# First h transposed ahead of the last score weights, x of pair 1 loaded by SyncE with its norm made beside the score matrix, column sums in a tile of their own

## The chip, the cores and the metric

The kernel runs on one core of one Trainium2 chip. The metric is the device time of one execution in microseconds (us), as the median of several runs. A profile is taken of one further execution; all moments given below are counted from the start of that execution's span.

## The reference

There are B = 128 graphs with N = 128 nodes and D = 512 features, all in float32. Two layers follow each other, each added to its input:

```
h = relu(layernorm(x))                                   # layer 0
Xw = h @ Wv + bv
e  = leaky_relu(Xw@aw[:d] over columns + Xw@aw[d:] over rows + ab, 0.2)
T  = adj * exp(e), each row divided by its sum
H  = h @ Wk[0] + bk[0] + (T h) @ Wk[1] + bk[1] + (T T h) @ Wk[2] + bk[2]
x  = x + relu(H)

h = relu(layernorm(x))                                   # layer 1
q, k = split(h @ Wqk);  v = h @ Wv1
w = mask/sqrt(512) * sum_d(q * (adj @ (k * mask)))
x = x + softmax_over_nodes(w) * v
```

Layer 1 needs q and k only in the product q·(adj k), so the kernel makes one 512 x 512 matrix Wq Wk^T ahead of everything else (the "score matrix") and uses it in place of the two.

## The kernel before, in words

Graphs are handled in 64 pairs (`G = 2`). For each pair p, layer 0 runs two block products after Strassen's scheme, seven products in place of eight (`strassen`, L371): `y2(p)` with the right side `r2` (Wk[2], with one column of attention weights on either side, 514 columns in all) and `y10(p)` with the right side `r10` (Wk[1] and Wk[0]). Their left side is h of the pair, transposed, and four sums of its blocks (`left_sums`). Their right side needs four differences of weight blocks each (`combine`, L191). Then come the two multiplications by the transition matrix (`inner`, `outer`), the layer norm of layer 1 (`norm2`) and the stores to DRAM that the second stage reads back. The second stage (from the closing of the first stage's buffers at L840) runs over quads of pairs and takes the last three eighths of the time.

The change touches the start, before the loop over pairs, and one choice in the loop.

**Loads.** SyncE (SP) issues x of pair 0, the four row chunks of Wqk (tile `tl`, 512 KB each), and the first two of four row blocks of Wv, Wk[2], Wk[1] and Wk[0] (`rows`, L166; tiles named `t`, `w`, `r` in the profile, 256 KB each, each filling 32 partitions). GpSimd (POOL) waits for chunk 1 of Wqk by means of a small copy, `gate` (L174), and then issues x of pair 1 and the other two row blocks of each matrix. Each queue also waits, before each issue, until an earlier transfer that used the same semaphore has landed. adj of pairs 0 and 1 comes last on both.

**TensorE (PE) up to the loop.** Two short warm-up groups; `weights_transposed` (L261), which transposes the four chunks of Wqk through six PSUM banks, each chunk into two banks of four transposes, copied out as `wqt` and `wkt`; `transposed_by_pe` (L351) for h of pair 0, through banks a2 and e2, which the chunks use as well; a transpose of the mask (`masks`), a small sum (`attention_constant`), the bias row spread over partitions (`bias`, bank c1); `score_matrix` (L276), 32 matmuls; `y2(0)`; two spreads of a column (L186); then `y10(0)` and the loop.

**VectorE (DVE) and ScalarE (ACT).** DVE makes the attention columns (`attention_columns`, L230), eight multiply-and-sum instructions over Wv, whose sums go straight into the two outer columns of `r2`, the tile that the loads of Wk[2] also fill. It then makes the differences for `r2`, the statistics of x of pair 1, and the differences for `r10`. ACT normalizes pair 1 (`norm0(1)`, L403, in two instructions at L316) as a step inside `y2(0)`, after its product 6. SP then stores h of pair 1 and reads it back in blocks.

**The order.** The program is written against a planner (Tile) that puts the instructions of each engine in an order of its own, from estimated times; the program pins it by hand where it wants: `tc.issue_after(done[...])`, `behind(...)` and `ordered(...)` (which chains PE instructions through `done["mm"]`) put an instruction behind a named earlier one of the same engine.

**One choice in the loop.** In `strassen` (L388) ACT copies bank a to bank b after the first product; the third product, on bank b, adds to that copy. The argument `second` names an instruction that this copy is put behind. In `y10(p)` (L600) it is `h2`, the last normalizing instruction of layer 1's norm of the pair before, for all p but the first and the last.

## Time and profile before

| what | us |
|---|---|
| runs of the kernel | 2225.20, 2225.92, 2229.39 (median 2225.92) |
| the profiled execution, its own time | 2229.96 |
| its span, first to last instruction | 2228.2 |
| PE busy in the span | 2205.7 (99%) |
| DVE, ACT, POOL busy | 1672.1, 1235.8, 698.6 |
| Wqk chunk 3 reaches PE | 13.35 |
| first score-matrix matmul | 16.78 |
| first matmul of y2(0) | 30.62 |
| first matmul of y10(0) | 38.52 |

The profile lists, for each instruction or run of like instructions, the start in us, the duration in us (of the whole run, where several are merged), the engine, the source line, the operation and its tiles as out<-in, the number of instructions, and in brackets how long the engine had been idle and what ended that. PE and PEld are matmuls and weight loads of TensorE; a matmul in float32 is listed as two. L91 and L86 are lines inside the helpers `ordered` and `behind`, so that many instructions stand under them. The words DMA, SPq and POOLq stand for transfers and for their issue.

### The profile page before, as it was taken

To read this page: it belongs to the slowest core of one execution; us is meant where nothing else is said; L and a number is where in the kernel's file an instruction comes from. 1 tells how busy PE (TensorE), PEld (TensorE's weight loads), DVE (VectorE), ACT (ScalarE), POOL (GpSimd) and SP (SyncE) were. 2 spreads that over 40 slices of the span, in tenths; PEclk is the share of its full clock that TensorE was granted. 3 is DMA by queue.
4 is the path that set the end of the run, shared out by engine and by line. 5 is a ranking of instruction groups with operands and counts; after the bars stand their busy time and mean duration, and the time that the engine had idled before them with its cause. 6 is when DMAs were issued, how large, how long until landed. Compare 5 with 4: busy or idle time off the path is not lost.

```text
span 2228.2 us, 29421 instructions
## 1 busy us (share of the span) xinstructions
PE 2205.7 (99%) x8113; PEld 1535.0 (69%) x8113; DVE 1672.1 (75%) x4529; ACT 1235.8 (55%) x2858; POOL 698.6 (31%) x822
## 2 busy tenths in 40 slices
PE   9999999999999999999999999999999999999998
PEld 5666665656666665666666666688888878887886
DVE  5778777778787777877778787587777767777777
ACT  4555554455554555545555554456666666666664
POOL 3111111111121211212112121245555555555454
PEclk9999999999999999999999999999999999999999
DMA  7688788888787887878778786668888888888876
GB/s 208 181 243 244 230 266 248 266 271 246 225 239 222 238 238 220 244 227 232 234 227 241 218 245 211 250 205 239 223 262 226 237 223 256 235 227 242 239 219 179
DMA packets 425615, 519.35 MB, mean 233 GB/s; under 512 B 100310, under 2 KB 281174, under 8 KB 409578
## 3 DMA queue, kind: packets, MB, share of 16 engines
q1 hardware_dynamic: 383880, 391.84, 58.1%
q0 software_dynamic: 41280, 125.09, 21.6%
q8 instruction: 65, 1.06, 0.2%
q14 instruction: 100, 0.82, 0.1%
q10 hardware_dynamic: 290, 0.53, 0.1%
HBM read 295.26 MB, written 222.07 MB: 232 GB/s over the span
## 4 chain that ended last, share of the span: by engine, by line
PE 90%; DVE 4%; DMA 3%; SPq 1%; ACT 1%; issue 1%; DVEq 0%
PE a L91 26%; PE c L91 24%; PE b L91 24%; PE e L91 15%; DMA td<-t 2%; DMA hv<-h2d 1%; SPq L534 1%; DVE st L290 0%; DMA tl<-in_L_gnn_Wqk_dram 0%; DVE fw L427 0%; DVE z L86 0%; SPq L342 0%; DVE x L621 0%; DMA xg<-in_x_dram 0%; SPq L86 0%
## 5 line engine op out<-in xcount | busy, mean ns | idle before, releaser
L669 POOL TENSOR_TENSOR c<-s,c 128x512 f32<-128x512 f32 (+1 forms) x186 | 201.0, 1094 | 250.2 <-DVE s L669 244.9
L111 POOL DMA_DIRECT2D agb<-in_adj_dram x256 | 149.7, 591 | 338.8 <-DVE aT L86 251.8
L91 PE MATMUL a<-r,x 128*128 128x512 f32 x512 | 242.4, 596 | 0.1
L91 PE MATMUL b<-rw,in 128*128 128x256 f32 x884 | 212.0, 379 | 0.0
L91 PEld LDWEIGHTS b<-rw,in 128*128 128x128 f32 x884 | 168.0, 190 | 23.3 <-issue 0.5
L435 POOL DMA_DIRECT2D fd<-fw x62 | 34.7, 559 | 464.3 <-DVE fw L443 278.0
L91 PEld LDWEIGHTS a<-r,x 128*128 128x128 f32 x512 | 97.6, 191 | 96.8 <-issue 93.4
L86 ACT COPY s<-c 128x257 f32<-128x257 f32 (+1 forms) x128 | 61.5, 481 | 173.4 <-PE c L91 173.2
L86 ACT COPY b<-a 128x257 f32<-128x257 f32 (+1 forms) x128 | 59.3, 464 | 171.6 <-PE a L91 171.6
L86 DVE TENSOR_TENSOR e<-e,s 128x512 f32<-128x512 f32 x64 | 44.7, 699 | 143.5 <-ACT s L86 143.5
L669 POOL TENSOR_TENSOR c<-c 128x1024 f32<-128x1024 f32 x61 | 144.1, 2362 | 11.2 <-DVE c L669 10.9
L91 PE MATMUL a<-w,x 128*128 128x257 f32 x512 | 131.9, 380 | 0.1
L91 PE MATMUL b<-w,sx 128*128 128x257 f32 x512 | 132.0, 380 | 0.0
L91 PE MATMUL b<-t,sx 128*128 128x512 f32 x256 | 120.4, 592 | 1.2 <-ACT b L86 1.2
L91 PE MATMUL c<-t,sx 128*128 128x512 f32 x256 | 120.5, 593 | 0.2
L91 PE MATMUL b<-r,sx 128*128 128x512 f32 x256 | 120.3, 592 | 0.0
L91 PE MATMUL e<-t,sx 128*128 128x512 f32 x256 | 120.3, 592 | 0.0
L91 PE MATMUL c<-t,x 128*128 128x512 f32 x256 | 120.3, 592 | 0.0
L669 DVE SCALAR_TENSOR_TENSOR junk<-agg,wscale,c 128x512 f32<-128x512 f32 x126 | 97.1, 770 | 29.9 <-POOL c L669 24.6
L669 ACT ACTIVATE c<-c,wcol 128x512 f32<-128x512 f32 x124 | 86.3, 720 | 56.7 <-DVE wcol L669 56.7
L427 DVE STREAM_TRANSPOSE fw<-hv 128x256 f32<-128x256 f32 x248 | 88.1, 413 | 30.1 <-DMA hv<-h2d 29.7
L91 PE MATMUL a<-rw,f 128*128 128x256 f32 x448 | 108.1, 379 | 0.0
(265 smaller groups left out, 5258.1 us busy)
## 6 DMA issues: line engine op xcount, KB each, us to landing
fd<-fw POOLq DMA_DIRECT2D x62, 1024.0 KB, 5.1
x1d<-x SPq DMA_DIRECT2D x64, 512.0 KB, 4.2
h2d<-h SPq DMA_DIRECT2D x64, 512.0 KB, 3.7
xg<-in_x_dram SPq DMA_DIRECT2D x63, 512.0 KB, 7.1
hd<-h SPq DMA_DIRECT2D x63, 512.0 KB, 3.6
hv<-hd SPq DMA_DIRECT2D x252, 128.0 KB, 4.2
hv<-h2d SPq DMA_DIRECT2D x248, 128.0 KB, 4.1
h<-h2d SPq DMA_DIRECT2D x62, 512.0 KB, 8.4
```

The source lines that it names most:

```text
L86: return op(*args, **how)
L91: done["mm"] = op(*args, **how).ins
L111: nc.gpsimd.dma_start(agb[p][c * S32:(c + 1) * S32].rearrange("p g q i -> p (g q) i"), v[c])
L427: done["c12"] = nc.vector.transpose(blocks[:, k, j].rearrange("p f (n b) -> p f n b", n=Q), hv[:, j].rearrange("p n (k f a) -> p k f n a", ...
L435: nc.gpsimd.dma_start(fd[:, half].rearrange("p o n -> p (o n)"), fv[:, half].rearrange("p o n -> p (o n)"))
L534: done["tv"] = nc.sync.dma_start(tv[c * S32:(c + 1) * S32].rearrange("p g q i -> p (g q) i"), v[c]).ins
L669: done[engine] = op(*args, **how).ins
```

## The change

- In the loads: SP issues x of pair 1 itself, right after the four chunks of Wqk and ahead of its weight rows; POOL no longer loads it, and its gate now waits for chunk 2 of Wqk.
- On PE: chunks 0 to 2 of Wqk are transposed first, then h of pair 0 (now in banks a1 and b1), the mask and the bias (now in bank b2), and only then chunk 3. All of these are now chained with `ordered`. Of the copies out of PSUM for `wkt`, ACT now does chunk 2 alone and DVE does chunks 0, 1 and 3.
- The statistics of x of pair 1 come on DVE behind the copies of the weights, and the norm (`norm0(1)`) behind the last copy of `wqt` on ACT, beside the score matrix; it is no longer a step of `y2(0)`. The differences for `r10` are put behind those for `r2`.
- The attention columns are put behind the left sums, their sums go to a new tile `ucol` (128 x 2 x 4), and two small copies, which are new, bring them into `r2`.
- In the loop, the copy in `y10(1)` is no longer put behind `h2`; for pair 2 and later it still is.

```diff
     for c in range(DC):
         nc.sync.dma_start(wqk_sb[:, c], wqk[c * P:(c + 1) * P])
+    load_x(1)
...
-    done["gate"] = nc.gpsimd.tensor_copy(gate, wqk_sb[:, 1, :1]).ins
+    done["gate"] = nc.gpsimd.tensor_copy(gate, wqk_sb[:, 2, :1]).ins
...
     with tc.issue_after(done["gate"]):
-        load_x(1, nc.gpsimd)
...
+        ucol = setup.tile([P, 2, DC], FP, name="ucol")
...
-                    junk, wv0_sb[:, f], 1.0, aw_bc[:, a, :], op0=OP.mult, op1=OP.mult, accum_out=r2[:, f, a * (W2 + HD):a * (W2 + HD) + 1]).ins
+                    junk, wv0_sb[:, f], 1.0, aw_bc[:, a, :], op0=OP.mult, op1=OP.mult, accum_out=ucol[:, a, f:f + 1]).ins
+        for a in range(2):
+            at = a * (W2 + HD)
+            done["u"] = behind("u", nc.vector.tensor_copy, r2[:, :, at:at + 1], ucol[:, a, :, None]).ins
...
-        nc.tensor.transpose(c1[:, :B], nm, ident[:B, :B])
+        ordered(nc.tensor.transpose, c1[:, :B], nm, ident[:B, :B])
...
-        nc.tensor.matmul(c1, ones[:K, :], bkr, start=True, stop=True)
-        nc.scalar.copy(bias_a[:, 1], c1[:, :HD])
-        nc.vector.tensor_sub(bias_e[:, 1], c1[:, HD:], bias_a[:, 1])
-
-    def weights_transposed():
+        ordered(nc.tensor.matmul, b2, ones[:K, :], bkr, start=True, stop=True)
+        nc.scalar.copy(bias_a[:, 1], b2[:, :HD])
+        nc.vector.tensor_sub(bias_e[:, 1], b2[:, HD:], bias_a[:, 1])
+
+    def weights_transposed(chunks):
...
-                    (nc.vector.tensor_copy if c < HC else nc.scalar.copy)(wkt[:, :, c * P:(c + 1) * P], pt)
+                    done["wk"] = (nc.scalar.copy if c == HC else nc.vector.tensor_copy)(wkt[:, :, c * P:(c + 1) * P], pt).ins
...
-            second="h2" if 0 < p < NP - 1 else "warm")
+            second="h2" if 1 < p < NP - 1 else "warm")
...
-    with tc.issue_after(done["vector"]):
-        weights_transposed()
+    done["mm"] = done["vector"]
+    weights_transposed(range(HC + 1))
     hT0 = lefts.tile([P, G, DC, N], FP, name="x")
-    transposed_by_pe(h0, hT0, (a2, e2))
+    transposed_by_pe(h0, hT0, (a1, b1))
     masks()
     behind("rs", attention_constant)
     bias()
-    attention_columns()
+    weights_transposed(range(HC + 1, DC))
+    rs1 = behind("wk", statistics, xg[1], "wq")
     LEFT[0] = left_sums(hT0)
-    with tc.issue_after(done["u"]):
-        right2 = combine(halves(r2, W2), [t2[:, i] for i in range(4)])
+    behind("left", attention_columns)
     for p in range(2):
         load_adj(p)
     for f in range(Q):
         score_matrix(f)
-    rs1 = behind("right", statistics, xg[1])
-    with tc.issue_after(done["rs"]):
+    behind("wq", norm0, 1, rs1)
+    with tc.issue_after(done["u"]):
+        right2 = combine(halves(r2, W2), [t2[:, i] for i in range(4)])
+    with tc.issue_after(done["right"]):
         right10 = combine(halves(r10, HD), pairs(t10))
     with tc.issue_after(done["right"]), tc.issue_after(done["m"]):
-        y2(0, {6: lambda: behind("s", norm0, 1, rs1)})
+        y2(0)
```

More of the change, by code (lines that the diff above doesn't have):

```diff
@@ L254, in bias @@
     def bias():
-        nc.tensor.matmul(c1, ones[:K, :], bkr, start=True, stop=True)
-        nc.scalar.copy(bias_a[:, 1], c1[:, :HD])
-        nc.vector.tensor_sub(bias_e[:, 1], c1[:, HD:], bias_a[:, 1])
-    def weights_transposed():
+        ordered(nc.tensor.matmul, b2, ones[:K, :], bkr, start=True, stop=True)
+        nc.scalar.copy(bias_a[:, 1], b2[:, :HD])
+        nc.vector.tensor_sub(bias_e[:, 1], b2[:, HD:], bias_a[:, 1])
+    def weights_transposed(chunks):
         banks = [a2, e2, a1, b1, c1, e1]
-        for c in range(DC):
+        for c in chunks:
             for a in range(2):
@@ L269, in weights_transposed @@
                     at = a * D + o * P
-                    nc.tensor.transpose(pt[:, o, :], wqk_sb[:, c, at:at + P], ident)
+                    ordered(nc.tensor.transpose, pt[:, o, :], wqk_sb[:, c, at:at + P], ident)
                 if a:
-                    (nc.vector.tensor_copy if c < HC else nc.scalar.copy)(wkt[:, :, c * P:(c + 1) * P], pt)
+                    done["wk"] = (nc.scalar.copy if c == HC else nc.vector.tensor_copy)(wkt[:, :, c * P:(c + 1) * P], pt).ins
                 else:
-                    nc.scalar.copy(wqt[:, :, :, c, :], pt.rearrange("p o (f a) -> p o f a", f=Q))
+                    done["wq"] = nc.scalar.copy(wqt[:, :, :, c, :], pt.rearrange("p o (f a) -> p o f a", f=Q)).ins
     def score_matrix(f):
@@ L355, in transposed_by_pe @@
             for f in range(Q):
-                nc.tensor.transpose(pt[:, f, :], h[:, j, f * P:(f + 1) * P], ident)
+                ordered(nc.tensor.transpose, pt[:, f, :], h[:, j, f * P:(f + 1) * P], ident)
             (nc.vector.tensor_copy if j else nc.scalar.copy)(dst[:, j], pt)
```

## The prediction

> **What bounds the kernel now.** I read the page first, then PE's waits, then the timeline around each wait that the diff touches.

> ```profile
> span 2228.2 us, 29421 instructions
> PE 2205.7 (99%) x8113; PEld 1535.0 (69%) x8113; DVE 1672.1 (75%) x4529; ACT 1235.8 (55%) x2858; POOL 698.6 (31%) x822
> ```

> PE is busy for all but 22.5 us. No edit takes work off PE, so the change can win only what it closes of those 22.5 us, and whatever is closed at the start moves all the rest forward. PE's waits, of the first 100 us and then of 250 to 450 us (total, times, longest, in us):

> ```profile
> PE a L270 <- DMA tl<-in_L_gnn_Wqk_dram: 1.4, 1, 1.4
> PE b L91 <- ACT b L86: 1.2, 1, 1.2
> ...
> PE a L186 <- ACT y L458: 1.0, 1, 1.0
> ```

> ```profile
> PE c L91 <- ACT s L86: 5.4, 4, 2.0
> PE a L91 <- DVE tt L86: 1.8, 2, 1.2
> ```

> The first three are the places that the diff touches, 3.6 us in all; the second fence is not touched. The first wait, in PE's timeline:

> ```profile
> 11.12 0.78 PE L270 MATMUL e<-ident,tl 128*128 128x128 f32 x4
> 13.35 0.63 PE L270 MATMUL a<-ident,tl 128*128 128x128 f32 x4 [1.44 <-DMA tl<-in_L_gnn_Wqk_dram]
> ...
> 14.25 0.27 PE L250 MATMUL c<-ident,nm 128*128 128x128 f32 x1
> 14.36 0.50 PE L245 MATMUL e<-ccol,ones 128*128 128x1 f32 x4
> 14.73 0.64 PE L356 MATMUL a<-ident,h 128*128 128x128 f32 x4
> 15.20 0.60 PE L356 MATMUL e<-ident,h 128*128 128x128 f32 x4
> 15.73 1.12 PE L257 MATMUL c<-bkr,ones 3*128 3x512 f32 x2
> 16.78 0.70 PE L280 MATMUL a<-wkt,wqt 128*128 128x512 f32 x1
> ```

> PE has nothing from 11.9 to 13.35, since chunk 3 of Wqk is late, and then does work that was ready long before (ACT finished h of pair 0 at 10.47). The other two waits, in ACT's part of the timeline:

> ```profile
> 36.27 1.52 ACT L316 ACTIVATE h<-xg,rs 128x512 f32<-128x512 f32 x2 [0.58 <-DVE rs L304]
> ...
> 37.69 0.35 ACT L458 COPY y<-c 128x257 f32<-128x257 f32 x1
> ...
> 38.10 0.32 PE L186 MATMUL a<-ident,y 128*128 128x128 f32 x1 [0.98 <-ACT y L458]
> ```

> ```profile
> 69.49 0.20 ACT L296 ACTIVATE r<-r 128x2 f32<-128x2 f32 x1
> 70.72 1.52 ACT L316 ACTIVATE h<-x,rs 128x512 f32<-128x512 f32 x2 [1.02 <-DVE rs L304]
> 72.14 0.58 ACT L86 COPY b<-a 128x512 f32<-128x512 f32 x1
> ```

> In both, ACT normalizes a pair for 1.52 us while PE waits for a copy queued behind it. The column sums on DVE:

> ```profile
> 21.51 0.69 DVE L235 SCALAR_TENSOR_TENSOR junk<-t,aw_bc 128x512 f32<-128x512 f32 x1 [2.99 <-DMA t<-in_L_gnn_Wv_dram]
> ...
> 24.50 0.69 DVE L235 SCALAR_TENSOR_TENSOR junk<-t,aw_bc 128x512 f32<-128x512 f32 x1 [2.29 <-issue]
> ```

> Wv is complete at 21.4; the second sum waits until the last row block of Wk[2] has landed (24.32), because it writes into the tile being loaded.

> [...] SP's transfers land in order of issue. [...] The row blocks fill 32 partitions each; [...] 206 GB/s from 10 to 14 us, when the rows run mostly from one queue, 276 GB/s from 14 to 30 us with two. [...] PE starts at half rate[...]. The trace shows it in durations: one group of four transposes starts every 0.86 us up to 11 us, and 0.46 us apart from 13.35; the idle 1.44 us did not slow it again.

> **The change part by part.**

> 1. *h, mask and bias ahead of chunk 3.* Before, from PE's restart to the score matrix: chunk 3 0.90 (13.35 to 14.25), mask 0.11, constant 0.37, h 1.00, bias 1.05, in all 3.43 us, to 16.78. After, PE goes on at about 11.9 (chunks 0 to 2 set this: they run at the cold rate without a gap), with banks a1 and b1 copied out by 11.42 and 11.2. Mask, h and bias take 2.16: 14.1. By then chunk 3 is there (13.35 before; nothing is put ahead of it). It takes 0.90: 15.0. But now its copies stand between it and the score matrix: the wkt copy on DVE takes 0.69 and some 0.2 to 0.3 for the two hand-overs (before, from the end of the last transpose's issue to the ACT copy 0.25): 15.95. Before, that copy hid behind h and bias. If the constant, 0.37, falls ahead of chunk 3 it is 16.3; in PE's new bubble of 0.95 it is free. Gain 16.78 - 15.95 = 0.85, ends 0.3 (a left sum of 0.42 runs on DVE when the copy is due, and the constant is ahead) and 1.3 (chunk 3 earlier, warm rate sooner). Taken: 0.9.
> 2. *Norm of pair 1 beside the score matrix.* ACT is idle from 17.3 to 20.5, beside the score matrix, so 1.52 + 0.50 for the logarithm and exponential fit there. In y2(0) the copy y<-c (0.35) then starts 0.2 after its product (36.83), at 37.03 in place of 37.69: gain 0.66 of the 0.98. The store and the four read-backs of h (0.37 + 1.80 us of issue on SP) come earlier; they wait behind SP's rows and adj in the ring and are needed only at 48.5, so they cost nothing; with that cover gone each us would be one us.
> 3. *Copy in y10(1) free of h2.* Product a ends at 69.74 by issue, the copy could start at 70.0 and ACT is idle from 69.69 to 70.72: a copy of 0.58 fits exactly. Gain 1.16; the norm behind it loses nothing. With the norm first after all, the 1.16 stays.
> 4. *x of pair 1 to SP, gate on chunk 2, ucol.* 512 KB move from POOL's ring to SP's, 2 us go by until POOL's gate opens (8.10 to about 10.2). POOL's first bytes came 5.8 us after its issue, and its ring then moved some 190 KB per us: Wv's 512 KB there by 19 at the latest, from 21.4. SP's half of Wv comes behind x of pair 1, at some 100 to 200 KB per us, by 18. Then DVE: eight sums of 0.73 = 5.9, two copies of 0.16 (nearest row: 128 x 4 at 0.16), four differences 2.63: done by 28 in place of 32.1. PE reaches y2(0) at about 29.7 (15.9 + 13.84), so none of it is on the path; the point at which it would be is Wv at 23.2. r10 landed last at 30.2; it is needed at 35.8, so POOL's two microseconds are covered by more than 5. Cost 0, ends -0.2 (a hand-over of DVE at 52.0 that PE just waits for goes away, since the r10 differences no longer run from 36.86 to 41.6) and +1.
> 5. *Rest.* `ordered`, the bank of the bias and the ucol tile add no instruction to PE. 0.2 gained for the hand-over at 52.0.

> Sum: 0.9 + 0.66 + 1.16 + 0.2 = 2.9 us. The profiled execution goes from 2229.96 (span 2228.2) to about 2227 (2225.3). That execution was 4.0 above the median of 2225.92; the saving is taken from the median: 2223.0, ratio 0.9987. Three runs spread over 4.2 us, and 0.2% (4.45 us) is about what a measurement of this kernel can tell from no change.

> **The rivals.** *B, one of the gains does not come.* The planner may still put the norm ahead of the copy in y10(1), since it stands ahead in the program and only the gap of 1.02 us makes room; or the constant and a left sum delay the score matrix. For it: nothing now pins that order. Against it: the copy was ready 0.7 us before the norm in the trace. Saving 1.2 to 2: about 2224.3. *C, more than the sum.* The waits at 250 to 450 us come from a round trip of the transition blocks through DRAM; they add to 7.2 us, and a moved start could shift them against the transfers. With two or three gone, 2219.5. Against it: they recur inside one pair's work, which the start doesn't change. *D, slower.* The same round trip, the other way: the planner orders the loop anew from its shifted start, and the wait of 1.2 us appears in more pairs. It decides from (2.9 + 4.45) / 1.2 = 6 to 7 further pairs; at ten it is 2225.9 - 2.9 + 12 = 2235. For it: six such waits exist already. Against it: the loop's order is pinned by hand, and between 80 and 260 us PE hardly waits.

> **How the numbers follow.** The sum as forecast 0.62, of which 0.15 falls beyond the bound by run spread and the upper ends of items 1 to 4; B 0.19; C 0.12; D 0.07. So faster by over 0.2% 0.27 (0.15 + 0.12), within 0.2% 0.66 (0.47 + 0.19), slower 0.07. The likeliest case has 2220.5 to 2225.5 for itself; with B and most of C the range is 2218.5 to 2227.

> **What would show it.** Right: no wait of `PE a L270` on tl; h's transposes (L356) before 13.5; the score matrix near 15.9 and y2(0) near 29.7; no wait of the spread above 0.4; no wait of `PE b L91` near 70; y10(1) some 1.7 us earlier, pair 2 some 2.9. Wrong: the score matrix at 16.3 or later, the norm still ahead of the copy, the last r2 difference after 30, or more waits on `ACT s` and `DVE tt` than six in the loop.

## The result, and the profile after

The changed kernel takes 2224.75 us at the median (14 runs, 2222.47 to 2227.22), the kernel before 2227.30 in the runs beside it (2225.20 to 2235.40). The ratio is put at 0.9984, 95% interval 0.9977 to 0.9992: 1.8 to 5.1 us less, in the middle 3.6, clear of no change. (The two medians lie 2.6 us apart, which is inside that interval.) Forecast were 0.9987 and 2223.0 us.

The page of the changed kernel, its first lines; PE is again busy all but 20 us:

```profile
span 2223.8 us, 29417 instructions
PE 2204.0 (99%) x8113; PEld 1535.0 (69%) x8113; DVE 1668.8 (75%) x4532; ACT 1236.0 (56%) x2857; POOL 697.9 (31%) x821
```

PE's waits in the first 100 us (total, times, longest, in us). The three that the prediction named are gone. The first line below stood there before too; the second is new:

```profile
PE e L221 <- DVE ones L158: 1.1, 1, 1.1
PE a L284 <- DVE wkt L276: 0.9, 1, 0.9
```

Between 250 and 450 us, which no edit touches, it waits as long as before (7.4 us, before 7.2), in more and shorter pieces:

```profile
PE c L91 <- ACT s L86: 7.1, 7, 1.5
PE a L91 <- DVE tt L86: 0.3, 1, 0.3
```

PE's timeline at the start, with the new order: h at 11.98, then mask, constant, bias, and chunk 3 at 14.47:

```profile
11.98 0.62 PE L91 MATMUL a<-ident,h 128*128 128x128 f32 x4
...
13.42 1.12 PE L91 MATMUL b<-bkr,ones 3*128 3x512 f32 x2
14.47 0.66 PE L91 MATMUL a<-ident,tl 128*128 128x128 f32 x4
14.96 0.60 PE L91 MATMUL e<-ident,tl 128*128 128x128 f32 x4
16.48 3.67 PE L284 MATMUL a<-wkt,wqt 128*128 128x512 f32 x8 [0.92 <-DVE wkt L276]
...
36.52 0.27 PE L186 MATMUL a<-ident,y 128*128 128x128 f32 x1
36.63 1.02 PE L91 MATMUL a<-r,x 128*128 128x512 f32 x2
37.49 0.27 PE L186 MATMUL a<-ident,y 128*128 128x128 f32 x1
37.60 1.02 PE L91 MATMUL a<-r,x 128*128 128x512 f32 x2
38.46 1.88 PE L91 MATMUL e<-t,sx 128*128 128x512 f32 x4
```

ACT's timeline beside the score matrix and at the end of y2(0): the norm of pair 1 is done long before the copy y<-c, which now starts 0.20 us after the first spread:

```profile
24.99 1.52 ACT L320 ACTIVATE h<-xg,rs 128x512 f32<-128x512 f32 x2 [3.54 <-DVE rs L308]
...
36.72 0.38 ACT L462 COPY y<-c 128x257 f32<-128x257 f32 x1 [1.36 <-PE c L91]
```

And at y10(1); the copy b<-a now goes ahead of the norm, into the gap that it had:

```profile
67.22 0.20 ACT L300 ACTIVATE r<-r 128x2 f32<-128x2 f32 x1
67.66 0.57 ACT L86 COPY b<-a 128x512 f32<-128x512 f32 x1 [0.24 <-PE a L91]
68.44 1.52 ACT L320 ACTIVATE h<-x,rs 128x512 f32<-128x512 f32 x2 [0.21 <-DVE rs L308]
```

Where the time came from, read as starts of the same PE instruction in the two profiles:

| PE instruction | before | after | gained so far | gained in this stretch |
|---|---|---|---|---|
| first of the score matrix | 16.78 | 16.48 | 0.30 | 0.30 |
| first of y2(0) | 30.62 | 30.29 | 0.33 | 0.03 |
| second product of y10(0) | 40.31 | 38.46 | 1.85 | 1.52 |
| first of y2(1) | 52.99 | 50.71 | 2.28 | 0.43 |
| first of y10(1) | 68.02 | 65.75 | 2.27 | -0.01 |
| third product of y10(1) | 72.77 | 69.18 | 3.59 | 1.32 |

So 3.6 us are gained by 73 us in these two profiles, in the middle of the measured interval. The spans differ by 4.4; the rest came and went in the loop and is treated in the last section. The first row is the least sure: the start up to the score matrix is the same in a second profile of the changed kernel and in four of the runs below, and in these six the score matrix begins between 16.05 and 16.81. The second profile of the changed kernel has 16.81 there, and its third product of y10(1) starts at 69.51, so that 3.3 us are gained by then. Of the kernel before there is one profile.

### The profile page after: what moved, and what is told of

Its sections match the earlier page's. It is cut to its first block, busy times and chain, and to the rows that moved or that the text cites. A ratio compares the mean times of both kernels' runs of the same rounds, so it can differ in the third digit from the quotient of the medians.

```text
span 2223.8 us, 29417 instructions
## 1 busy us (share of the span) xinstructions
PE 2204.0 (99%) x8113; PEld 1535.0 (69%) x8113; DVE 1668.8 (75%) x4532; ACT 1236.0 (56%) x2857; POOL 697.9 (31%) x821
## 4 chain that ended last, share of the span: by engine, by line
PE 90%; DMA 4%; DVE 4%; SPq 1%; issue 1%; ACT 1%; DVEq 0%; ACTq 0%
PE a L91 26%; PE c L91 24%; PE b L91 24%; PE e L91 15%; DMA td<-t 2%; DMA hv<-h2d 2%; SPq L538 1%; DVE st L294 1%; DVE fw L431 1%; SPq L346 0%; DVE x L625 0%; DVE z L86 0%; DMA h2d<-h 0%; DMA xg<-in_x_dram 0%; PE a L284 0%
## 5 line engine op out<-in xcount | busy, mean ns | idle before, releaser
L91 PE MATMUL a<-r,x 128*128 128x512 f32 x512 | 240.8, 592 | 0.0
L91 PE MATMUL b<-rw,in 128*128 128x256 f32 x884 | 212.0, 379 | 0.0
L91 PEld LDWEIGHTS b<-rw,in 128*128 128x128 f32 x884 | 168.0, 190 | 23.3 <-issue 0.5
L91 PEld LDWEIGHTS a<-r,x 128*128 128x128 f32 x512 | 97.0, 190 | 95.7 <-issue 92.3
L86 ACT COPY s<-c 128x257 f32<-128x257 f32 (+1 forms) x128 | 61.5, 481 | 173.3 <-PE c L91 173.2
L86 ACT COPY b<-a 128x257 f32<-128x257 f32 (+1 forms) x128 | 59.3, 464 | 168.9 <-PE a L91 168.9
L86 DVE TENSOR_TENSOR e<-e,s 128x512 f32<-128x512 f32 x64 | 44.7, 698 | 142.6 <-ACT s L86 142.6
L673 POOL TENSOR_TENSOR c<-c 128x1024 f32<-128x1024 f32 x61 | 144.1, 2362 | 11.2 <-DVE c L673 10.8
L91 PE MATMUL a<-w,x 128*128 128x257 f32 x512 | 131.9, 380 | 0.1
L91 PE MATMUL b<-w,sx 128*128 128x257 f32 x512 | 132.0, 380 | 0.0
L91 PE MATMUL c<-t,sx 128*128 128x512 f32 x256 | 120.5, 593 | 0.2
L91 PE MATMUL e<-t,sx 128*128 128x512 f32 x256 | 120.3, 592 | 0.0
L91 PE MATMUL b<-t,sx 128*128 128x512 f32 x256 | 120.3, 592 | 0.0
L91 PE MATMUL c<-t,x 128*128 128x512 f32 x256 | 120.3, 592 | 0.0
L91 PE MATMUL b<-r,sx 128*128 128x512 f32 x256 | 120.3, 592 | 0.0
L91 PE MATMUL a<-rw,f 128*128 128x256 f32 x448 | 108.1, 379 | 0.0
```

The lines of the kernel that those rows point to most:

```text
L86: return op(*args, **how)
L91: done["mm"] = op(*args, **how).ins
L673: done[engine] = op(*args, **how).ins
```

## The experiments

What was in doubt: whether h ahead of chunk 3 made the first gain (the theory of the prediction) or the loads did; whether the second gain is the norm's or the new order on PE; and whether the edits costed at nothing were nothing. Most comparisons are made by moments of the profile, since one microsecond is less than the runs of a kernel differ by.

**The copy behind h2 again.**

```diff
-            second="h2" if 1 < p < NP - 1 else "warm")
+            second="h2" if 0 < p < NP - 1 else "warm")
```

> The changed kernel with the copy in y10(1) put behind h2 again; only ACT's order differs. Theory: the norm (two instructions, 1.52 us) stands ahead of the copy again, PE waits 1.1 to 1.3 us at its third product of y10(1) (start near 70.4 in place of 69.18), and all later moments are later by as much, the first wait after 250 us at 282.4 in place of 281.2. Rival (the shifted start lets the norm end in time anyway): no wait there, 69.2.

Measured: PE's timeline and then ACT's, of this run:

```profile
70.54 1.98 PE L91 MATMUL b<-t,sx 128*128 128x512 f32 x4 [1.15 <-ACT b L86]
```

```profile
68.49 1.52 ACT L320 ACTIVATE h<-x,rs 128x512 f32<-128x512 f32 x2 [1.02 <-DVE rs L308]
69.92 0.57 ACT L86 COPY b<-a 128x512 f32<-128x512 f32 x1
```

From the first to the third product of y10(1) it takes 4.74 us (before 4.75, changed 3.43). The theory holds at this place, with a wait of 1.15 us as expected. But the whole execution took 2225.22 us against 2225.62 for the changed kernel's profiled one: the waits between 280 and 420 us were shorter in this run by more than the 1.3 us. The first of them came at 282.6, as expected; the end of a single execution can't show an edit of this size.

**The loads alone, on the kernel before.**

```diff
         nc.sync.dma_start(wqk_sb[:, c], wqk[c * P:(c + 1) * P])
+    load_x(1)
...
-    done["gate"] = nc.gpsimd.tensor_copy(gate, wqk_sb[:, 1, :1]).ins
+    done["gate"] = nc.gpsimd.tensor_copy(gate, wqk_sb[:, 2, :1]).ins
...
-        load_x(1, nc.gpsimd)
```

> The kernel before, with x of pair 1 on SP behind Wqk and the gate on chunk 2, and nothing else. Theory of the prediction (chunk 3 lands as before, the order on PE makes the gain): PE waits for chunk 3 until 13.3, score matrix at 16.8. Rival (the loads alone bring chunk 3 in earlier, since no weight rows run beside it): chunk 3 by 11.4 to 11.7, wait on tl under 0.2 us, score matrix at 15.3 to 15.6, earlier than the 16.48 of the changed kernel.

PE's timeline of this run:

```profile
11.75 0.63 PE L270 MATMUL a<-ident,tl 128*128 128x128 f32 x4 [0.20 <-DMA tl<-in_L_gnn_Wqk_dram]
...
15.18 3.27 PE L280 MATMUL a<-wkt,wqt 128*128 128x512 f32 x7
```

The rival holds: with PE's old order the wait for chunk 3 falls from 1.44 to 0.20, and the score matrix starts 1.6 us before that of the kernel before and 1.3 before that of the changed kernel. Further on this run waits where the changed one doesn't: 0.9 for a copy by ACT in y2(0), 0.5 at the spread, 1.1 in y10(1). So at the second product of y10(0) (39.75) it is only 0.56 ahead of the kernel before, and the changed kernel is 1.85 ahead: most of what the loads give is lost again without the other edits.

**The gate alone, and x of pair 1 alone.** The two load edits apart: first the gate on chunk 2, with x of pair 1 still on POOL; then x of pair 1 on SP, with the gate still on chunk 1.

> The kernel before, with the gate on chunk 2 alone; x of pair 1 stays on POOL. If POOL's traffic held chunk 3 up: it lands by 11.7 and the score matrix starts before 15.7. If SP's own weight rows behind it did: 13.2 and 16.8 as before.

> The kernel before with x of pair 1 on SP behind Wqk, gate still on chunk 1. If x of pair 1, as a full-width transfer between Wqk and the rows on SP's ring, is what brings chunk 3 early: chunk 3 by 11.7 and the score matrix near 15.2 as with both load edits. If the later gate is needed too: chunk 3 after 12.5, score matrix after 16.

The gate alone gave 2236.94 us in its first run: chunk 2 was late (PE got it at 12.18) and chunk 3 later than ever. PE's timeline:

```profile
12.18 1.12 PE L270 MATMUL c<-ident,tl 128*128 128x128 f32 x4 [1.70 <-DMA tl<-in_L_gnn_Wqk_dram]
...
15.97 1.09 PE L270 MATMUL a<-ident,tl 128*128 128x128 f32 x4 [1.82 <-DMA tl<-in_L_gnn_Wqk_dram]
...
22.51 6.56 PE L280 MATMUL a<-wkt,wqt 128*128 128x512 f32 x8
```

Both waits together are 3.5 us, but y2(0) starts 8.6 us later than in the kernel before, since PE stayed at half rate: the first eight listed score matmuls take 6.56 us in place of 3.70. A second run of it was timed.

> The kernel before with the gate on chunk 2 alone, again and timed. If the first run's 2237 was chance (chunks 2 and 3 land at different moments in each execution of the kernel before): median within 2 us of before, score matrix mostly at 16.8. If the gate itself costs: about 9 us above before in every run, PE at half rate until some 28 us.

Its median is 2230.77 (20 runs), ratio 1.0013, interval 1.0006 to 1.0020: slower by 2.5 to 3 us, not 9. In its profile chunk 3 was there by 12.02 without a wait, so the late chunks of the first run were chance. What costs is another thing. PE's waits in the first 100 us:

```profile
PE e L91 <- DVE w L191: 2.4, 1, 2.4
PE b L91 <- ACT b L86: 1.1, 1, 1.1
```

DVE's timeline has the differences for r2 at 32.27 in place of 29.53, because POOL's rows of Wv and Wk[2], which stand behind x of pair 1 and now behind a later gate, come later:

```profile
32.27 2.63 DVE L191 TENSOR_TENSOR w<-w 128x514 f32<-128x514 f32 x4
```

With x of pair 1 on SP and the old gate, PE found chunk 3 at 11.66 without a wait (it had landed at 11.34), and the score matrix began at 15.12, as with both edits:

```profile
11.66 0.60 PE L270 MATMUL a<-ident,tl 128*128 128x128 f32 x4
...
15.12 3.27 PE L280 MATMUL a<-wkt,wqt 128*128 128x512 f32 x7
```

PE came to full rate in this run at 11.3 and in the kernel before at 11.5 (there its transposes went from 421 to 273 ns each), so the clock does not make this difference. The gate adds nothing here; it is the move of x of pair 1, from POOL to the place right behind Wqk on SP, that goes with an early chunk 3. In all eleven profiles with x of pair 1 there, chunk 3 landed between 10.9 and 11.6; in the three without, PE got it at 12.02 or before, 13.35 and 15.97. With one of those three in time, how often chunk 3 is late in the kernel before is not known, nor therefore what the loads gain in a typical execution.

POOL's loads cannot be what made the last two late, for the first packets of x of pair 1 came at 14 us in the kernel before and at 19.7 in the late run. What differs up to then is what follows Wqk on SP's ring, and the packet records of the traces fit that as the cause. Between 11 and 12 us the 2 KB packets of SP's queue took 0.08 us (median) in each of the eleven profiles, where they are mostly those of x of pair 1, but 0.17, 0.27 and 0.24 us in the other three, where they are weight rows. The last three packets of Wqk, 4 KB each, took 0.16 to 0.30 us in the eleven; in the three they took 0.28 to 0.31 (in time), 0.41 to 0.53 and 0.47 to 0.50 (the two late ones). That is a part of the lateness only: in the kernel before, the last of them ended at 11.76 and PE went on at 13.35, while in the changed kernel the last ended at 11.10 and chunk 3 had landed at 11.41. No run changed the shape of the rows alone, so that their 32 partitions are the reason is not shown.

**PE's old order on the changed kernel,** in one profiled run and then timed beside the changed kernel itself.

```diff
-    weights_transposed(range(HC + 1))
+    weights_transposed(range(DC))
...
-    transposed_by_pe(h0, hT0, (a1, b1))
+    transposed_by_pe(h0, hT0, (a2, e2))
...
-    weights_transposed(range(HC + 1, DC))
```

> The changed kernel with all four chunks transposed first and h, mask and bias after them, as before; loads and all else as changed. Theory of the prediction (h ahead of chunk 3 is what wins): the score matrix no earlier than 16.5. Rival (with chunk 3 landed at 11.4 there is nothing left to fill, and chunk 3 last on PE leaves its copies uncovered): no wait on tl, none on wkt, score matrix at 15.3 to 15.6, y2(0) at 29.2 to 29.5 in place of 30.29.

> The changed kernel with the transposes of all four chunks ahead of h, mask and bias, as before; timed. By the moments of its first profile (y10(0) 1.23 us ahead of the changed kernel): 1.2 us below the changed kernel, ratio to before near 0.9978. If the further 2.5 us that its profile gained between 242 and 486 us are lasting, 3.7 below, ratio 0.997.

> The changed kernel itself, timed beside the others on one chip: ratio to before 0.9984 as recorded; start moments as in its profile (score matrix 16.5, y10(1) third product 69.2).

PE's timeline of the first run; no wait on tl and none on wkt:

```profile
11.66 0.60 PE L91 MATMUL a<-ident,tl 128*128 128x128 f32 x4
...
14.17 1.12 PE L91 MATMUL b<-bkr,ones 3*128 3x512 f32 x2
15.22 3.27 PE L284 MATMUL a<-wkt,wqt 128*128 128x512 f32 x7
```

The rival holds here too. The same PE work, from the end of chunk 2 to the score matrix, takes 3.56 us (11.66 to 15.22) against 4.50 in the changed kernel (11.98 to 16.48) and 3.43 after its wait in the kernel before. The second product of y10(0) starts at 37.23 and, in the timed run's own profile, 37.59, against 38.46 and 38.79. Part of such differences is the moment at which PE came to full rate: 11.3 and 12.0 with the old order, 12.0 and 12.7 in the two profiles of the changed kernel. The two with 12.0 start the score matrix at 15.59 and 16.48, so 0.9 us is what chunk 3 in last place costs. The second profile of the changed kernel missed what was expected of it: its score matrix starts at 16.81 in place of 16.5, no earlier than in the kernel before.

Timed, the old order has ratio 0.9977 (0.9967 to 0.9987, median 2223.37 of 8), the changed kernel 0.9984 again (0.9977 to 0.9990, median 2224.24 of 21). The old order beats the kernel before. That it beats the changed kernel by about 0.9 us is shown by the profiles; the intervals of the times overlap, and the medians are 0.9 apart, the means 1.5. The times do not settle whether any of the further 2.5 us of its first profile is lasting: a ratio of 0.997 lies within the interval.

**Chunk 3 ahead of the bias,** with h still first (the line that transposes chunk 3 moved up to stand ahead of `attention_constant` and `bias`). PE's timeline of this run stands below the expectation.

> The changed kernel with chunk 3 ahead of the bias and the constant (h, mask, chunk 3, constant, bias); h still comes first. Theory (what costs in the changed kernel is that the copies of chunk 3 have no cover): the wait on wkt of 0.92 us goes, score matrix at 15.4 to 15.7. Rival (h ahead of chunk 3 costs by itself): 16 or later.

```profile
11.48 0.66 PE L91 MATMUL a<-ident,h 128*128 128x128 f32 x4 [0.32 <-ACT wqt L278]
...
12.51 0.60 PE L91 MATMUL a<-ident,tl 128*128 128x128 f32 x4
...
13.82 1.12 PE L91 MATMUL b<-bkr,ones 3*128 3x512 f32 x2
14.87 3.70 PE L284 MATMUL a<-wkt,wqt 128*128 128x512 f32 x8
```

Even earlier than expected, in part since PE got its full rate at 9.7 in this execution and at 12.0 in the changed kernel's. What doesn't depend on that: from h to the score matrix 3.39 us in place of 4.50, and the wait on wkt is gone. h first costs no more than the 0.32 us for which PE waits there until its bank is copied out; it is the copies of the last chunk, with no PE work behind them, that cost about 1 us in the changed kernel.

**The norm back in y2(0), and the spreads back ahead of y10(0).** Two undoings for the second gain. In the first the norm is a step after product 6 again (`y2(0, {6: ...})`), in the second the two spreads are chained with `ordered`:

```diff
-        spread_columns(0)
+        for j in range(G):
+            ordered(nc.tensor.transpose, PZ[0][:, j, :], Y2[0][:, j, 0, :1].to_broadcast([P, P]), ident)
```

> The changed kernel with the norm of pair 1 again a step of y2(0), its statistics still early. Theory: ACT's 1.52 us stand before a copy that PE waits for; from the first matmul of y2(0) to the second product of y10(0) it takes 8.9 to 9.7 us in place of 8.17, with a wait of 0.5 to 1 us at a copy by ACT. Rival (the gain at this place is only that PE's spreads are now interleaved with the first product of y10(0)): 8.2 to 8.4.

> The changed kernel with both spreads of y2(0)'s column pinned ahead of y10(0), as they stood before; the norm stays beside the score matrix. Theory of the prediction (the copy that is no longer behind the norm makes the gain, 0.66): PE waits 0.3 to 0.4 us for the copy, 8.9 to 9.1 us from the first matmul of y2(0) to the second product of y10(0), in place of 8.17 now and 9.69 before. Rival (the interleaving is nothing): 8.2 to 8.4.

From the first matmul of y2(0) to the second product of y10(0) the two take 8.69 and 9.07 us (before 9.69, changed 8.17). PE's timeline of the first:

```profile
30.48 1.03 PE L91 MATMUL a<-w,x 128*128 128x257 f32 x4
...
34.53 1.14 PE L91 MATMUL c<-w,sx 128*128 128x257 f32 x4 [0.25 <-ACT c L86]
...
39.17 1.88 PE L91 MATMUL e<-t,sx 128*128 128x512 f32 x4
```

And of the second, where y2(0) starts at 30.06 and the second product of y10(0) at 39.13:

```profile
36.29 0.27 PE L91 MATMUL a<-ident,y 128*128 128x128 f32 x1
36.92 0.32 PE L91 MATMUL a<-ident,y 128*128 128x128 f32 x1 [0.35 <-ACT y L462]
37.34 1.96 PE L91 MATMUL a<-r,x 128*128 128x512 f32 x4
```

So of the 1.52 us gained here, 0.62 come from the norm being gone from ahead of the copy (9.69 to 9.07), the sum's 0.66, and 0.90 from an order that the diff doesn't write: the planner put half of y10(0)'s first product between the two spreads. With the norm back but that order kept, 0.52 is lost, of which 0.25 is a wait for a copy by ACT in y2(0); 8.69 lies between what the theory (8.9 and more) and the rival (8.4 and less) had led to expect.

**No ucol.** The sums go into r2 again, without the two copies.

> The changed kernel with the column sums written into r2 again, without the tile ucol and its two copies. Expected by all: the second sum waits for the last row block of Wk[2] (near 23.9), the differences for r2 end near 32 in place of 30.06. Theory (cover): y2(0) starts at 30.3 and PE waits no more than 0.3 us in it. Rival (the tile is what makes room for the earlier y2(0)): 1 us or more of waiting in y2(0).

DVE's timeline; the second sum waits for Wk[2] again, but the differences start 0.6 later only (27.42 in the changed kernel):

```profile
22.97 0.69 DVE L235 SCALAR_TENSOR_TENSOR junk<-t,aw_bc 128x512 f32<-128x512 f32 x1 [1.21 <-DMA w<-in_L_gnn_Wk_dram]
...
27.99 2.63 DVE L191 TENSOR_TENSOR w<-w 128x514 f32<-128x514 f32 x4
```

PE has no wait in y2(0), which starts at 29.86. In this one profile the tile is worth nothing; the differences ended at 30.62, not 32.

## Why the prediction was right, and where it was not

The time, the direction and the case forecast (within 0.2%, about 2.9 us less) held; the middle of the measured interval is 3.6 us less. That the sum came so near is in part luck: item 1 fell short by 0.6 us, and 0.90 us came in at item 2 that no item had foreseen. Of the prediction's own signs of being wrong three came true: the score matrix started after 16.3 (16.48), the last r2 difference ended after 30 (30.06), and there were eight waits on `ACT s` and `DVE tt` in place of six. The first cost the 0.6 us; r2 cost no wait, and the eight waits together 0.2 us more than the six. By its steps:

1. *h, mask and bias ahead of chunk 3: forecast 0.9, measured 0.30, and for another reason* (between nothing and 0.7 in the six profiles that share this start). The step that failed is "by then chunk 3 is there (13.35 before; nothing is put ahead of it)". That sentence reckons only with what stands ahead of chunk 3 in the ring. (SP's transfers do land in order of issue: of those whose landing the trace of the kernel before gives, at 5.63, 10.16, 14.31, 23.33, 28.22 and 33.15 us.) With x of pair 1 moved in behind it, it landed near 11.4, and the loads alone bring the score matrix 1.6 us forward with PE's old order. With that there was no wait left for the reordering to fill. It only took the cover from chunk 3's copies and lost 0.9 to 1.3. The lower end of 0.3 was named with two causes. One came: the constant ran ahead of chunk 3 (0.44 us). The other did not matter: a left sum ended at 15.74 as the copy was due, but the copy began at 15.65, 0.25 us after the last transpose's issue (15.40), as had been counted. What the new order is worth where chunk 3 is late, as the prediction supposed, no run shows.
2. *Norm beside the score matrix: forecast 0.66, measured 0.62 by undoing, and 0.90 beside it.* Mechanism and size were right, though the norm ran at 24.99 and not in the gap from 17.3 to 20.5, since DVE did its short steps for it between the column sums. Missing was a term for what the planner does with PE's order when its inputs come earlier.
3. *Copy free of h2: forecast 1.16, measured 1.32.* Right in mechanism and place; of rival B the norm ahead of the copy did not happen, while its other case, the constant ahead of chunk 3, did (item 1).
4. *Loads and ucol at no cost: right that they cost nothing, but the loads' gain was not seen (item 1).* The cover was named rightly: r2's differences ended at 30.06, not by 28, but PE did not wait. The later gate by itself does cost, through the late r2 (2.4 us of wait, 1.0013); the change escapes it because x of pair 1 leaves POOL's ring.
5. *Hand-over at 52: forecast 0.2, measured 0.43* from the second product of y10(0) to y2(1). No run undid this by itself.

Rival C's waits in the loop were in the changed profile as long as before (7.4 and 7.2 us), and D did not happen.

## What to carry to other kernels

When a transfer that the start hangs on is late, look at what the same queue issues behind it too; here a full-width transfer there went with a landing at 10.9 to 11.6 us in eleven profiles, and narrow weight rows with a late one (13.35 and 15.97) in two of three. When work is moved to fill a wait, first see whether the same change removes the wait, and keep independent work behind the last transposes, so that their copies out of PSUM have cover. At an edit of a microsecond, read moments of the same instruction in two profiles; the end of a single run cannot show it. Compare profiles in which PE came to full rate at the same moment, or stretches that begin after it: in the six profiles with the same start, that moment lay between 10.9 and 12.7 us, and the score matrix came later by up to 0.8 us with it.

## What the runs showed of the hardware

A wait of PE can cost more than itself. In the kernel before, a wait of 2.04 us ended at 331.46, and the clock's records have it at 0.50 of the full one from 332.34 to 335.75. In a line of the view by windows stand the window, its length, the busy us of PE, PEld, DVE, ACT and POOL with the number of instructions, the granted TensorE clock as a share of the full one (here 0.50), the DMA share and GB/s. The timeline has a first product of 3.50 us in place of 1.88:

```profile
332.40:335.70 3.30, 3.30 (x5) 1.38 (x5) 3.23 (x10) 1.72 (x4) 1.59 (x3) 0.50 0.94 313
...
336.00:340.00 4.00, 4.00 (x11) 1.75 (x10) 2.31 (x6) 2.23 (x5) 0.00 (x0) 1.00 0.87 297
```

```profile
331.46 1.26 PE L91 MATMUL c<-w,x 128*128 128x257 f32 x4 [2.04 <-ACT s L86]
332.51 3.50 PE L91 MATMUL a<-r,x 128*128 128x512 f32 x4
```

That is some 1.7 us lost. It is part of the 4.4 us between the two spans: PE's busy time fell by 1.7 us (2205.7 to 2204.0), though no edit takes work off PE, and its idle time by 2.7. The gate alone, timed, shows the same after its wait of 2.35 us:

```profile
33.30:36.60 3.30, 3.30 (x9) 2.56 (x9) 2.98 (x7) 0.37 (x1) 0.58 (x1) 0.50 0.36 68
```

A wait that was hardly shorter did not do this. With the norm back, PE waited 2.01 us and went on at the full rate:

```profile
374.62 1.13 PE L91 MATMUL c<-w,x 128*128 128x257 f32 x4 [2.01 <-ACT s L86]
375.60 1.88 PE L91 MATMUL a<-r,x 128*128 128x512 f32 x4
```

At the start PE was at about half rate: in the kernel before a transpose began every 0.21 us until 11.5, and from 13.35 every 0.11, and the first record of the clock, at 1.00, begins at 11.49 (in the changed kernel at 12.01). This moment differed between executions, 9.7 to 12.7 us, and was 28.3 where PE waited twice for Wqk (1.70 and 1.82 us). In the kernel before, PE had worked almost without a gap from 1.09 us on. What sets the moment these runs do not show.
